# A message-passing kernel on one core: third parts of messages on another engine, an earlier x load, and normalisation in single steps

## The chip, the cores and the metric

The kernel runs on one core of a Trainium2 chip. The metric is the device time of one execution in microseconds. A core has TensorE (PE, matmuls; PEld is its weight load), VectorE (DVE), ScalarE (ACT), GpSimd (POOL) and SyncE (SP). The first four compute, each through its own queue in program order. SyncE, ScalarE and GpSimd issue the DMAs here.

## The reference

There are 6250 nodes with 128 features and 100000 edges, sorted by destination. Each edge has one of two types, and its message is the source row times one of two weight matrices plus a bias. Messages are summed at the destination, the node's own product is added, and ReLU, residual and a layer norm follow:

```
Xs = X[src]
m_data = Xs @ W_data.T + b_data
m_ctrl = Xs @ W_control.T + b_control
msg = jnp.where((edge_types == 0)[:, None], m_data, m_ctrl)
agg = jax.ops.segment_sum(msg, dst, num_segments=X.shape[0])
out = agg + (X @ W_self.T + b_self)
x = layernorm(x + relu(out))          # eps 1e-5, over 128 features
```

## The kernel before

**Table of messages.** Since a message depends only on source and type, the kernel computes all of them once. Nodes stand in 49 blocks of 128. For each block `multiply` (lines 457 to 466) makes y = x w + bias in fp32 in PSUM, 256 columns for the two types. Two blocks share a PSUM bank (a "pair", 25 in all), and four banks rotate. The f32 value is then split into three bf16 parts that add up to it: `take` (lines 471 to 474) copies the sum to bf16 on ScalarE, and `leave` (476 to 482) subtracts the copy from the PSUM sum on TensorE, with a matmul by minus the identity. So each pair goes y, yh (high copy), y1 (subtract), ym (middle copy), y2 (subtract), yl (low copy). Three copies of a pair on ScalarE and two subtractions for each block on TensorE are needed. The parts stay in SBUF as m3 and are stored to DRAM as table.

**Edges.** SyncE loads a sample of edges (r), from which VectorE, TensorE and a gather (er) find the first edge of each block. Then SyncE loads a window of edges for each block (line 372), after it has read the start from the tile first. Blocks are taken in two ways. The first 35, in seven groups of five, use selection by matmuls: `edge_fields` computes fields on VectorE, `bucket_hots` makes one-hot tiles hot_st (line 548), and in `ranks` TensorE and VectorE take turns for 18 steps: a matmul with tri, a max reduction into slot (line 565), a matmul with rest. `fill_a` and `fill_b` turn slots into lists (hr, two, then small at line 602). The lists go through DRAM (packed) and come back to all partitions as rows; VectorE compares them (line 727). From there TensorE gathers messages by matmuls with m3 (g_ps, line 756), ScalarE evicts them (gs, line 771) and TensorE adds them into agg by a one-hot matmul with hot_d. The other 14 blocks take their messages from the table by GpSimd's gathers (msg, line 857), which need all stores of the table; they are added into agg_g.

**Order.** `Order.run` is a planner that works while the program is built. Each stream yields steps with a price for each engine that may take it, and with needs. The planner puts the step that can start first, by due time, into the program. When a step has two engines, the one that would start first takes it. The prices and due times thus decide the order in which instructions stand in each engine's queue. On the chip the queues run by themselves.

**End of a block.** `finish_blocks` sums the three parts, adds x and takes statistics. `normalise` (from line 812) does this for a group of up to five blocks: square root on ScalarE, reciprocals on VectorE, then `apply` (lines 188 to 191), one ScalarE activation per block, all five as one step priced at 0.28 us each, and a store. `sums_over_all` is a fallback that runs only when the counts don't match all edges.

The loads at the start are bias and then w on ScalarE's queue (lines 241 and 243). x comes in seven parts (4, 8, 8, 8, 8, 8 and 5 blocks), through `load_x` on ScalarE's queue (line 452).

Of the kernel before, what the change touches and what calls it, by code (L numbers as in the profile page):

```python
# [9 lines left out]
F32 = mybir.dt.float32  # L10
# [9 lines left out]
P = 128  # L20
D = 128
# [79 lines left out]
def step(name, costs, *needs, lag=0.0):  # L101
    return as_tuple(name), costs, [as_tuple(n) for n in needs], lag
# [7 lines left out]
def kernel(  # L110
# [74 lines left out]
                                       op0=ALU.mult, op1=ALU.mult)  # L185
        return rstd, shift

    def apply(h, rstd, shift, n):
        for j in range(n):
            nc.scalar.activation(h[:, j, :], h[:, j, :], AF.Identity,  # L190
                                 bias=shift[:, j : j + 1], scale=rstd[:, j : j + 1])

    def store_out(h, b0, n, by=nc.sync):
        n0 = b0 * P
# [20 lines left out]
def sums_over_windows(ctx, tc, x, xt, edges, w, bias, table, packed, total,  # L215
# [21 lines left out]
    early = ctx.enter_context(ExitStack())  # L237
    build = early.enter_context(tc.tile_pool(name="build", bufs=2))
    ps_y = early.enter_context(tc.tile_pool(name="ps_y", bufs=YB, space=PSUM))
    b1 = build.tile([1, D3], F32, name="b1", bufs=1)  # L240
    A.dma_start(b1, bias)
    w_sb = const.tile([D, D3], F32, name="w_sb")
    A.dma_start(w_sb, w)


    iota_f = const.tile([P, 640], F32, name="iota_f")
# [46 lines left out]
        in_offset=bass.IndirectOffsetOnAxis(ap=row_i[:, 0:1], axis=0),  # L293
    )

    order.free.update(V=7.0, T=6.5, G=8.0)


    pid1 = const.tile([P, 1], F32, name="pid1")
# [74 lines left out]
            )  # L374


    xts, ys = {}, {}
    at_part = [sum(PARTS[:g]) for g in range(len(PARTS))]
    two_blocks = [(g, b, min(2, at_part[g] + n - b))
                  for g, n in enumerate(PARTS) for b in range(at_part[g], at_part[g] + n, 2)]  # L380


    LEAD, BUILT = 8.0, 76
    BLOCK = 13.1
    PACE = 1.68
    AHEAD, FIRST = 26.0, 20
# [60 lines left out]
    def load_x():  # L447
        for g, n in enumerate(PARTS):
            free = [("y", at_part[g - 1] - 1)] if g > 1 else []
            yield step(("xt", g), {"A": 0.45}, *free, lag=3.5)  # L450
            xts[g] = build.tile([D, max(PARTS), P], F32, name="xt")[:, :n]
            A.dma_start(xts[g].rearrange("p b c -> p (b c)"),
                        xt[:, at_part[g] * P : (at_part[g] + n) * P])

    def multiply():
        for i, (g, b, n) in enumerate(two_blocks):
            for j in range(n):
                free = [("yl", two_blocks[i - YB][1])] if i >= YB and j == 0 else []
                yield step(("y", b + j), {"T": 0.97}, ("xt", g), *free)
                if j == 0:  # L460
                    y = ys[b] = ps_y.tile([P, 2, 2 * D], F32, name="y")
                T.matmul(y[:, j, :], xts[g][:, b + j - at_part[g], :], w_sb[:, : 2 * D],  # L462
                         start=j == 0, stop=False, skip_group_check=True)
                T.matmul(y[:, j, :], ones_b, bias3[:, : 2 * D], start=False, stop=True, skip_group_check=True)  # L464
# [10 lines left out]
    def leave(i, kind, after):  # L475

        for g, b, n in two_blocks:
            yield step((kind, b), {"T": 0.11 * n}, (after, b))
            for j in range(n):
                T.matmul(ys[b][:, j, :].rearrange("p (t c) -> p t c", t=2), minus,  # L480
                         m3v[:, :, b + j, i * D : (i + 1) * D], start=False, stop=True,
                         skip_group_check=True)

    def store():
        for g, n in enumerate(PARTS):
# [305 lines left out]
    def own_of(blocks, begun):  # L791

        for i, b in enumerate(blocks):
            yield step(("agg", b), {"S": 0.0}, *([("whole", blocks[i - 1])] if i else []))
            yield step(("o", b), {"T": 0.5}, ("xs", b), begun(b))
            by_columns(aggs[b][:, :D], x_ts.pop(b), w_sb[:, 2 * D :], start=False, stop=False,
                       skip_group_check=True)
            by_columns(aggs[b][:, :D], ones_b, bias3[:, 2 * D :], start=False, stop=False,
                       skip_group_check=True)
# [16 lines left out]
    def normalise(pieces, last):  # L816

        for grp, (get, b0, q0, n) in enumerate(pieces):
            yield step((last, "root", grp), {"V": 0.2}, ("sum", b0 + n - 1))
            h, mv = get()  # L820
            h, mv = h[:, q0 : q0 + n, :], mv[:, q0 : q0 + n, :]
            v, s0 = root(mv, n, work)
            yield step((last, "rooted", grp), {"A": 0.3}, (last, "root", grp))
            yield step((last, "scale", grp), {"V": 1.0}, (last, "rooted", grp))
            scales = scale(mv, v, s0, n, work)
            yield step((last, "apply", grp), {"A": 0.28 * n}, (last, "scale", grp))
            apply(h, *scales, n)
            at_end = last == "p" and grp == len(pieces) - 1
            yield step((last, "out", grp), {"A": 0.4} if at_end else {"S": 0.3}, (last, "apply", grp))
            store_out(h, b0, n, nc.scalar if at_end else nc.sync)  # L830


# [75 lines left out]
    def close_build():  # L908
# [8 lines left out]
        spread(), select(), finish_blocks(),  # L917
        normalise([(lambda g=g: (hs_[g], mvs[g]), STARTS[g] + q0, q0, n) for g, q0, n in PIECES], "p"), add_up(), gather(), evict(), to_hots(), bucket_hots(),
        multiply(), take(0, "yh", "y"), leave(0, "y1", "yh"),
        take(1, "ym", "y1"), leave(1, "y2", "ym"), take(2, "yl", "y2"), constants(), store(), close_build(), add_counts(),  # L920
        finish_gathered(), gathered_sums(), gathered_hots(), gather_rows(), gathered_fields(),
        normalise([(lambda i=i: kept[i], NPB + i * GQ, 0, min(GQ, NG - i * GQ))
                   for i in range(-(-NG // GQ))], "g"),
# [8 lines left out]
def sums_over_all(ctx, tc, xt, edges, w, bias, table, dram, finish, load_rows, norm):  # L932
# [69 lines left out]
    for b0 in range(0, NB, Q):  # L1002
# [12 lines left out]
            finish(h[:, j, :], s_in, load_rows(b0 + j, work))  # L1015
            stats(mv[:, j, :], h[:, j, :], work)
        v, s0 = root(mv, n, work)
        apply(h, *scale(mv, v, s0, n, work), n)
        store_out(h, b0, n)


# [29 lines left out]
```

## Time and profile before

| | us |
|---|---|
| median of three runs | 545.55 |
| lowest, highest | 544.28, 546.7 |
| profiled execution | 628.27 |
| its span | 626.6 |
| TensorE busy in it | 550.4 |
| VectorE busy | 429.4 |
| ScalarE busy | 424.7 |
| GpSimd busy | 292.8 |

The profiled execution is longer than the runs by 82.7 us. Times inside the profile are from the start of the span. The start-up, in which the message parts and the first group's lists are made, ends when the first gather matmul starts, at 79.98 us. The main stage lasts from there to about 612 us, and the rest is the last group. In a line of a timeline the columns are start, duration, engine, line of the kernel, operation, output and inputs, shape and count; in brackets stands how long the engine was idle before it, and what released it.

### The profile page before, as it was taken

To read this page: it belongs to the slowest core of one execution; us is meant where nothing else is said; L and a number is where in the kernel's file an instruction comes from. 1 tells how busy PE (TensorE), PEld (TensorE's weight loads), DVE (VectorE), ACT (ScalarE), POOL (GpSimd) and SP (SyncE) were. 2 spreads that over 40 slices of the span, in tenths; PEclk is the share of its full clock that TensorE was granted. 3 is DMA by queue.
4 is the path that set the end of the run, shared out by engine and by line. 5 is a ranking of instruction groups with operands and counts; after the bars stand their busy time and mean duration, and the time that the engine had idled before them with its cause. 6 is when DMAs were issued, how large, how long until landed. Compare 5 with 4: busy or idle time off the path is not lost.

```text
span 626.6 us, 26397 instructions
## 1 busy us (share of the span) xinstructions
PE 550.4 (88%) x11222; PEld 441.2 (70%) x11222; DVE 429.4 (69%) x962; ACT 424.7 (68%) x1008; POOL 292.8 (47%) x267
## 2 busy tenths in 40 slices
PE   5899888896989898897988989999999998888994
PEld 3555466675768686786877877788777787666783
DVE  4767677567667777776787766877686667446784
ACT  6755555565587666777767676786767876676684
POOL 1000026654465556655556464665646554554400
PEclk9999988999899999999999999999999999999998
DMA  3567754324243433435333433443344542534300
GB/s 108 168 196 221 249 188 128 117 66 158 58 127 123 127 111 117 136 109 152 93 128 114 142 122 106 127 144 106 122 133 119 157 152 68 161 103 146 106 18 27
DMA packets 60932, 79.19 MB, mean 126 GB/s; under 512 B 15760, under 2 KB 51371, under 8 KB 60807
## 3 DMA queue, kind: packets, MB, share of 16 engines
q1 hardware_dynamic: 47109, 48.88, 24.3%
q0 software_dynamic: 12400, 25.08, 14.3%
q10 hardware_dynamic: 1298, 3.48, 1.6%
q8 instruction: 89, 1.46, 0.9%
q14 instruction: 36, 0.29, 0.1%
HBM read 64.35 MB, written 13.05 MB: 124 GB/s over the span
## 4 chain that ended last, share of the span: by engine, by line
PE 80%; ACT 7%; issue 5%; DVE 4%; DMA 2%; SPq 1%; another core or an unknown queue 0%; POOL 0%; ACTq 0%; DVEq 0%; POOLq 0%
PE agg L232 27%; PE g_ps L756 26%; PE acc L232 8%; PE agg_g L232 8%; PE small L602 7%; ACT gs L771 5%; PE y L462 2%; ACT h_p L190 1%; DMA rows<-packed 1%; DVE slot L565 1%; PE y L480 1%; DVE hot_st L548 1%; ACT h_g L190 1%; PE y L464 0%; DMA xt<-in_xt 0%
## 5 line engine op out<-in xcount | busy, mean ns | idle before, releaser
L771 ACT CAST gs<-g_ps 128x384 bf16<-128x384 f32 x804 | 337.2, 494 | 151.3 <-PE g_ps L756 97.4
L857 POOL DMA_INDIRECT msg<-table,idx x252 | 283.1, 1124 | 208.0 <-PE g_ps L756 90.5
L756 PE MATMUL g_ps<-m,rows 128*32 128x384 bf16 x3430 | 330.8, 334 | 19.2 <-ACT gs L771 11.6
L232 PE MATMUL agg<-gs,hot_d 128*32 128x384 bf16 x3360 | 304.4, 338 | 27.8 <-ACT gs L771 12.9
L232 PEld LDWEIGHTS <-hot_d 128*32 128x32 bf16 x3500 | 198.9, 137 | 66.7 <-issue 56.4
L756 PEld LDWEIGHTS <-rows 128*32 128x32 bf16 x3430 | 185.5, 138 | 46.4 <-issue 40.6
L565 DVE TENSOR_REDUCE slot<-acc 128x5 bf16<-128x490 f32 x126 | 83.8, 665 | 75.5 <-PE acc L232 39.7
L232 PE MATMUL agg_g<-msg,hot_g 128*32 128x384 bf16 x1008 | 107.2, 330 | 1.2 <-issue 1.1
L741 DVE TENSOR_TENSOR hot_d<-count,to 128x1664 bf16<-128x1664 bf16 x70 | 74.7, 1068 | 21.7 <-PE agg L232 12.8
L602 PE MATMUL small<-hot_st,two 128*32 128x98 bf16 x1260 | 70.9, 290 | 1.4 <-issue 1.3
L602 PEld LDWEIGHTS <-two 128*32 128x32 bf16 x1260 | 56.8, 118 | 6.7 <-issue 4.6
L232 PE MATMUL acc<-hot_st,rest 128*32 128x490 bf16 x476 | 55.1, 380 | 6.1 <-DVE slot L565 5.0
L232 PE MATMUL acc<-hot_st,tri 128*32 128x490 bf16 x504 | 58.8, 376 | 1.0 <-DVE hot_st L548 0.9
L473 ACT CAST m<-y 128x512 bf16<-128x512 f32 (+1 forms) x75 | 40.6, 580 | 25.7 <-PE y L480 18.0
L232 PEld LDWEIGHTS <-hot_g 128*32 128x32 bf16 x1008 | 51.4, 125 | 4.9 <-issue 3.0
L548 DVE TENSOR_TENSOR hot_st<-count,st_b 128x2940 bf16<-128x2940 bf16 x21 | 41.9, 1997 | 13.7 <-PE small L602 5.4
L696 POOL DMA_INDIRECT mixed<-table,row_i x7 | 7.4, 1055 | 87.3 <-PE g_ps L756 81.2
L727 DVE TENSOR_SCALAR rows<-rows,pid 128x3136 bf16<-128x3136 bf16 x35 | 36.3, 1038 | 3.3 <-DMA rows<-packed 3.3
L153 DVE TENSOR_REDUCE whole<-agg 128x128 f32<-128x384 f32 x35 | 19.4, 553 | 27.5 <-PE g_ps L756 23.4
L462 PE MATMUL y<-w_sb,xt 128*128 128x256 f32 x98 | 31.6, 409 | 1.7 <-DMA xt<-in_xt 1.7
L232 PEld LDWEIGHTS <-rest 128*32 128x32 bf16 x476 | 20.9, 99 | 16.0 <-issue 15.3
L771 DVE CAST gs<-g_ps 128x384 bf16<-128x384 f32 x36 | 19.3, 554 | 13.7 <-PE g_ps L756 12.2
(140 smaller groups left out, 423.6 us busy)
## 6 DMA issues: line engine op xcount, KB each, us to landing
rows<-packed SPq DMA_DIRECT2D x35, 784.0 KB
table<-m SPq DMA_DIRECT2D x10, 768.0 KB
msg<-table,idx POOLq DMA_INDIRECT x252
xt<-in_xt ACTq DMA_DIRECT2D x5, 512.0 KB
xt_p<-in_xt SPq DMA_DIRECT2D x35, 64.0 KB
xs_p<-in_x SPq DMA_DIRECT2D x35, 64.0 KB
out<-h_p SPq DMA_DIRECT2D x6, 320.0 KB
table<-m SPq DMA_DIRECT2D x2, 480.0 KB
```

Source lines behind the costliest of these rows:

```text
L153: nc.vector.tensor_reduce(whole, agg.rearrange("p (i c) -> p c i", i=3), axis=AX.X, op=ALU.add)
L232: T.matmul(out[c : c + 32], lhsT[:, c : c + 32], rhs, **flags)
L462: T.matmul(y[:, j, :], xts[g][:, b + j - at_part[g], :], w_sb[:, : 2 * D], start=j == 0, stop=False, skip_group_check=True)
L473: A.copy(part_of(b, n, i), ys[b][:, :n, :].rearrange("p b (t c) -> p t b c", t=2))
L548: V.tensor_tensor(hot, counted[n][:, None, 1 : NT + 1, :].to_broadcast([P, KC, NT, n]), fields[grp][2][:, c * KC : c * KC + KC, None, :].t ...
L565: V.tensor_reduce(slots[grp][:, k, :], by_q, axis=AX.X, op=ALU.max)
L602: T.matmul(vt[c0 : c0 + R, q // 2, :], two[:, k % KC, i, :, q], hot[:, k % KC, :, q], start=k == 0 and q < 2, stop=k == KT - 1, skip_group ...
L727: V.tensor_scalar(rows[b], rows[b], pid1, None, op0=ALU.is_equal)
L741: V.tensor_tensor(hot, counted[DC][:, :, :n], places[grp][:, q, None, c * DC : c * DC + n].to_broadcast([P, P, n]), op=ALU.is_equal)
L756: T.matmul(g_ps[t * R : (t + 1) * R, :D3], rows[b][:, :, s], m3[:, s, :], start=True, stop=True)
L771: (A.copy if e == "A" else V.tensor_copy)(gs[at], g_tiles.pop((b, g))[at, :D3])
L857: G.indirect_dma_start(out=msgs[j, k], out_offset=None, in_=table[:, :], in_offset=bass.IndirectOffsetOnAxis(ap=idx[:, j, k : k + 1], axis=0),
```

## The change

Four things are changed.

1. `leave` and `take` for the third part become `last_part`. For each pair the planner chooses. Either one VectorE tensor_sub reads the PSUM sum and the middle part and writes the third part, or, as before, TensorE subtracts and ScalarE copies. In the built program 9 of the 25 pairs go to VectorE.
2. The first part of x is loaded on SyncE's queue, second after r. w is loaded ahead of the bias on ScalarE's queue.
3. `apply` takes one block, and each one is a step of its own, priced at 0.39 us.
4. Prices and times of the planner: TensorE is free from 5.0 instead of 6.5, LEAD is 6.0 instead of 8.0, a y block costs 1.0 instead of 0.97, and a block's own product 0.25 instead of 0.5.

```
-    def apply(h, rstd, shift, n):
-        for j in range(n):
-            nc.scalar.activation(h[:, j, :], h[:, j, :], AF.Identity,
-                                 bias=shift[:, j : j + 1], scale=rstd[:, j : j + 1])
+    def apply(h, rstd, shift, j):
+        nc.scalar.activation(h[:, j, :], h[:, j, :], AF.Identity,
+                             bias=shift[:, j : j + 1], scale=rstd[:, j : j + 1])
...
+    w_sb = const.tile([D, D3], F32, name="w_sb")
+    A.dma_start(w_sb, w)
+    xts = {0: build.tile([D, max(PARTS), P], F32, name="xt")[:, : PARTS[0]]}
+    nc.sync.dma_start(xts[0].rearrange("p b c -> p (b c)"), xt[:, : PARTS[0] * P])
     b1 = build.tile([1, D3], F32, name="b1", bufs=1)
     A.dma_start(b1, bias)
-    w_sb = const.tile([D, D3], F32, name="w_sb")
-    A.dma_start(w_sb, w)
...
-    order.free.update(V=7.0, T=6.5, G=8.0)
+    order.free.update(V=7.0, T=5.0, G=8.0)
...
-    LEAD, BUILT = 8.0, 76
+    LEAD, BUILT = 6.0, 76
...
-            yield step(("xt", g), {"A": 0.45}, *free, lag=3.5)
+            yield step(("xt", g), {"A": 0.45} if g else {"S": 0.0}, *free, lag=3.5 if g else 0.0)
+            if not g:
+                continue
...
-                yield step(("y", b + j), {"T": 0.97}, ("xt", g), *free)
+                yield step(("y", b + j), {"T": 1.0}, ("xt", g), *free)
...
+    def last_part():
+
+        for g, b, n in two_blocks:
+            by = yield step(("y2", b), {"T": 0.11 * n, "V": 0.13 + 0.275 * n}, ("ym", b))
+            sums = ys[b][:, :n, :].rearrange("p b (t c) -> p t b c", t=2)
+            if by == "V":
+                V.tensor_sub(part_of(b, n, 2), sums, part_of(b, n, 1))
+            else:
+                for j in range(n):
+                    T.matmul(ys[b][:, j, :].rearrange("p (t c) -> p t c", t=2), minus,
+                             m3v[:, :, b + j, D : 2 * D], start=False, stop=True,
+                             skip_group_check=True)
+            yield step(("yl", b), {"A": 0.16 + 0.21 * n} if by == "T" else {"S": 0.0}, ("y2", b))
+            if by == "T":
+                A.copy(part_of(b, n, 2), sums)
...
-            yield step(("o", b), {"T": 0.5}, ("xs", b), begun(b))
+            yield step(("o", b), {"T": 0.25}, ("xs", b), begun(b))
...
-            yield step((last, "apply", grp), {"A": 0.28 * n}, (last, "scale", grp))
-            apply(h, *scales, n)
+            for j in range(n):
+                yield step((last, "apply", grp, j), {"A": 0.39}, (last, "scale", grp))
+                apply(h, *scales, j)
...
-        take(1, "ym", "y1"), leave(1, "y2", "ym"), take(2, "yl", "y2"), constants(), store(), close_build(), add_counts(),
+        take(1, "ym", "y1"), last_part(), constants(), store(), close_build(), add_counts(),
```

More of the change, by code (lines that the diff above doesn't have):

```diff
@@ L374, in starts @@
             )
-    xts, ys = {}, {}
+    ys = {}
     at_part = [sum(PARTS[:g]) for g in range(len(PARTS))]
@@ L825, in normalise @@
             scales = scale(mv, v, s0, n, work)
-            yield step((last, "apply", grp), {"A": 0.28 * n}, (last, "scale", grp))
-            apply(h, *scales, n)
+            for j in range(n):
+                yield step((last, "apply", grp, j), {"A": 0.39}, (last, "scale", grp))
+                apply(h, *scales, j)
             at_end = last == "p" and grp == len(pieces) - 1
-            yield step((last, "out", grp), {"A": 0.4} if at_end else {"S": 0.3}, (last, "apply", grp))
+            yield step((last, "out", grp), {"A": 0.4} if at_end else {"S": 0.3}, (last, "apply", grp, n - 1))
             store_out(h, b0, n, nc.scalar if at_end else nc.sync)
@@ L1017, in sums_over_all @@
         v, s0 = root(mv, n, work)
-        apply(h, *scale(mv, v, s0, n, work), n)
+        scales = scale(mv, v, s0, n, work)
+        for j in range(n):
+            apply(h, *scales, j)
         store_out(h, b0, n)
```

## The prediction

> **What bounds the kernel now.** I read the page first, then the chain of waits, then the start-up (the first 80 us) by timeline, because nearly all of the edit lies there.
>
> ```profile
> span 626.6 us, 26397 instructions
> PE 550.4 (88%) x11222; PEld 441.2 (70%) x11222; DVE 429.4 (69%) x962; ACT 424.7 (68%) x1008; POOL 292.8 (47%) x267
> PE 80%; ACT 7%; issue 5%; DVE 4%; DMA 2%; SPq 1%; another core or an unknown queue 0%; POOL 0%; ACTq 0%; DVEq 0%; POOLq 0%
> ```
>
> TensorE carries 80% of the chain that ended last, so work taken off another engine is worth only what TensorE waits for it. TensorE's own work that the edit removes is in the start-up. This is that stage in stretches of 10 us (columns: length, busy PE, PEld, DVE, ACT, POOL, granted clock, DMA share, GB/s):
>
> ```profile
> 10.00:20.00 10.00, 9.61 (x59) 6.86 (x58) 1.72 (x11) 8.00 (x17) 0.00 (x0) 1.00 0.48 133
> 20.00:30.00 10.00, 8.43 (x62) 5.19 (x60) 9.79 (x22) 6.88 (x14) 0.00 (x0) 1.00 0.55 154
> 40.00:50.00 10.00, 9.93 (x115) 5.62 (x113) 7.55 (x10) 6.71 (x12) 0.00 (x0) 1.00 0.75 229
> 70.00:80.00 10.00, 7.00 (x62) 3.45 (x64) 7.14 (x24) 4.88 (x10) 0.00 (x0) 0.95 0.87 290
> ```
>
> So three limits follow each other: from 18.4 to 30.7 us VectorE (9.79 of 10), then TensorE until 68, then, in 70 to 80, the DMA engines and VectorE, with TensorE idle 3 of 10. The timelines show both hand-overs. VectorE at the first and the last one, and TensorE's wait between:
>
> ```profile
> 18.41 0.32 DVE L515 TENSOR_TENSOR rel_b<-win,base 128x90 bf16<-128x90 int32 x1 [6.03 <-DMA win<-in_edges]
> 20.84 3.90 DVE L548 TENSOR_TENSOR hot_st<-count,st_b 128x2940 bf16<-128x2940 bf16 x2
> 32.78 0.67 DVE L565 TENSOR_REDUCE slot<-acc 128x5 bf16<-128x490 f32 x1 [0.73 <-PE acc L232]
> 75.18 1.04 DVE L727 TENSOR_SCALAR rows<-rows,pid 128x3136 bf16<-128x3136 bf16 x1 [1.58 <-DMA rows<-packed]
> 77.54 1.04 DVE L727 TENSOR_SCALAR rows<-rows,pid 128x3136 bf16<-128x3136 bf16 x1 [0.75 <-DMA rows<-packed]
> 78.50 0.66 DVE L565 TENSOR_REDUCE slot<-acc 128x5 bf16<-128x490 f32 x1
> ```
> ```profile
> 22.89 0.39 PE L232 MATMUL acc<-hot_st,tri 128*32 128x490 bf16 x4 [0.89 <-DVE hot_st L548]
> 79.21 0.60 PE L232 MATMUL acc<-hot_st,rest 128*32 128x490 bf16 x4 [1.44 <-DVE slot L565]
> ```
>
> The second fence says that the first rank matmul waits for VectorE, and that the last one before the gathers begin (first g_ps at 79.98) waits for a slot reduction which stands in VectorE's queue behind the selection of the second block's rows, and so behind a DMA.
>
> **What the Trainium skill says.** "VectorE: DVE Perf Modes", the TRN2 errata section and the perf-mode tier table: an operation from PSUM costs about 120 cycles plus its elements at 0.96 GHz, and tensor_tensor with a PSUM operand runs at one element a cycle. For 512 elements that is an estimate of 0.66 us. The trace is slightly above the formula: 490 elements from PSUM took 0.667 (formula 0.635), so I take 0.69, of which 0.62 shows as spacing. "DMA: Bandwidth & Descriptors", "Issuing engines are not separate DMA queues": moving a load to another issuing engine saves issue time only. The trace of before has no such pair to compare. [...] Here DMA traffic ends at about 86 us and the first table gather is issued at 88.32, 2.3 us later. "TensorE: Matmul & The Clock Gate", Part 1: the first 3.4 us or so of activity run at half clock. Here a y matmul pair goes from 0.85 us at 9.47 to 0.43 at 11.43, with the step near 10.5, 3.5 us after the start; an earlier start brings the same cold stretch with it.
>
> **The change part by part.** Sums are on the profiled execution, 628.27 us (span 626.6). The median of the runs shown is 545.55, 82.7 less, so profiling stretches the kernel; I carry absolute differences over, and scaled by 545.55/628.27 = 0.87 they would be a little smaller.
>
> x and w. The first x load leaves ScalarE's queue (issued at 4.16 behind the bias copies, landed 6.87) for SyncE's, behind the r load that takes 1.0 us to issue. With the 2.7 us that it took, it lands near 4.5 to 5.3; TensorE is held by begun until 4.92 + 0.3, so y starts at about 5.4 instead of 7.00. It is one DMA, and SyncE's next instruction is only at 12.4 (it waited 10.6 us for first), so nothing behind it is late. b now follows w in ScalarE's queue: about 0.4 us later, hence the parts on VectorE, begun, er. That is hidden: first_f was ready at 10.03 and first waited 2.15 us for TensorE's queue; without this cover +0.4. The 1.5 us head start goes into a wait: the first rank matmul already waits 0.89 us for hot_st. Worth 0; bounds -1.5 and +0.4.
>
> Two early subtractions. In the built program one stands on VectorE ahead of first, one between the fields and the first hot_st. The first needs the second pair's middle part; I place ScalarE's copy at 11.2 to 11.8, so first ends about 0.2 later. Behind it are SyncE's window loads and all of group 0. The second delays hot_st, on the chain, by 0.62. Together +0.8 (bounds 0 and +1.6).
>
> Fewer subtractions on TensorE. 9 of 25 pairs go to VectorE: 98 to 80 minus matmuls, 18 less. Between the rank step at 30.7 and the last L602 of group 0 there are 44 of them before and 32 after, with 21 y blocks in both. In the chain a pair is 0.22 alone and 0.32 next to acc, so 0.13 each: 12 x 0.13 = -1.6 (bounds -1.3, -1.9). The nine ScalarE casts that go (0.58 each) are hidden: ScalarE idles 25.7 us before its L473 casts.
>
> Five subtractions among the rank steps. Each takes 0.62 of VectorE; a step leaves VectorE idle 0.70 to 0.89 (0.73 above). They fit when their copy is there; one stands directly before hr and two (2.2 us), where nothing is idle. +0.4 (bounds 0 and +3). Slots ready, packed and the rows loads therefore: 0.8 - 1.6 + 0.4 = -0.4.
>
> The start of the gathers. In the new order the slot that the last rest needs, and also hr, two and the first hot_d, stand behind the first block's rows only; the second rows selection comes after two hot_d. Before: 77.54 + 1.04, slot 0.66, acc at 79.21. After: 75.18 + 0.95, slot, about 76.8. That is -2.4 for g_ps, and -2.3 for the first agg (hot_d ends at 80.0 instead of 82.3). What is late next: the gathered messages. POOL's table gathers begin at 88.32, when the stores have landed, msg 0 at 89.50; TensorE takes it at 92.72 and would now be there at 90.3. The DMA share is 0.9 to 1.1 from 72 to 86, so the stores don't land sooner. I credit -1.6 (bounds -2.4 and 0).
>
> Single normalisation steps. Five applies run together 2.04 us on ScalarE, ahead of evictions, and TensorE then waits 1.1 to 1.24 us (186.36, 264.13, 574.22). The planner's price goes from 0.28 to 0.39, the spacing that they have. In the built program evictions come between applies in four of the ten runs of five or four (1+4, 1+4, 1+1+2, 1+3); six runs of five stay whole, though planned. Three or four applies still stand together, so I take 0.3 for each of the four: -1.2 (bounds -3 and 0). The new prices of y and o and the earlier start add no instruction; they reorder TensorE by a few tiles: 0, bounds -2 and +2. The fallback's apply isn't executed.
>
> Sum: -0.4 - 1.6 - 1.2 = -3.2, so 628.3 becomes 625.1 profiled, and 545.55 becomes 542.3.
>
> **The rivals.** First: the message gathers take the place of the wait removed (the -1.6 becomes 0) and half the normalisation gain is lost: -0.4 - 0.6 = -1.0, about 544.6. For it: the 2.4 us between where TensorE would be and where it was. Against: TensorE in 90 to 98 is idle 3.4 of 8 us by "issue", which no gather explains. Second, on the other side: VectorE becomes the bound of the start-up. A subtraction waits for ScalarE's copy at the head of VectorE's queue, the slot behind it is late, then TensorE's rest and tri. Price: 9 x 0.62 = 5.6, less 1.6, so +4: 549.5. It decides once the copy is more than 0.1 us later than the slot before it, since 0.73 of idle less 0.62 is all there is. For it: DVE 9.79 of 10 in 20 to 30. Against: 7.55 in 40 to 50 leaves 2.5 us for about two subtractions. Third: the head start is kept, because y is further on at each rank step, and the gate and the applies give all that they have: -1.5, -0.8 and -1.8 more than the sum, about 538. The edit can't fail to do what it says: the built program shows nine subtractions and the moved load.
>
> **How the numbers follow.** Main case 45%, 542.3 (own range 539.5 to 544.5); gathers 20%, 544.6; VectorE bound 15%, 549.5; more gain 20%, 538. About 0.5%, 2.7 us, is what a measurement of this kernel can tell, so faster means under 542.8: somewhat over half of the main case and all of the last, 0.26 + 0.20 = 0.46. Same: the rest of the main case and nearly all of the gathers, 0.19 + 0.18 = 0.37. Slower: 0.15 + 0.02 = 0.17. The range leaves out part of both outer cases: 536.0 to 548.5.
>
> **What would show it.** First y matmul near 5.4; first rank matmul near 23.5 with a longer wait for hot_st; packed within 1 us of 68.8; first g_ps near 77 to 78; nine subtractions of 0.69. Wrong: slot reductions with waits for ScalarE casts ahead of them, TensorE under 9 of 10 between 30 and 68, a wait of 2 us at the first agg_g, or a main stage (80 to 612) that changes by more than 2 us either way.

## The result and the profile after

| | before | after |
|---|---|---|
| median of five runs, us | 546.52 | 542.67 |
| lowest, highest | 544.28, 546.7 | 542.34, 543.6 |
| ratio, 95% interval | | 0.9939 [0.9911, 0.9966] |

The medians are 3.85 us apart; the ratio of 0.9939 is 3.3 us (1.9 to 4.9). The forecast was 542.3. The total came out nearly as worked out, but most of its parts did not.

First a mistake about the profile of before. I had said that profiling stretches the kernel by 82.7 us. The changed kernel's profiled execution took 542.67 us, exactly its median:

```profile
span 540.9 us, 26355 instructions
PE 507.3 (94%) x11204; PEld 442.9 (82%) x11204; DVE 432.4 (80%) x967; ACT 415.9 (77%) x1003; POOL 297.4 (55%) x267
PE 73%; DMA 9%; ACT 5%; DVE 5%; issue 3%; SPq 3%; POOL 1%; ACTq 0%; DVEq 0%; POOLq 0%
```

So the profile doesn't stretch anything. In the experiments the kernel before, unprofiled, took 636.5 to 637.2 us on two chips, 630.4 on a third and 548.0 on a fourth. The first profile of before (628.27) is of the longer kind, the times shown beside it are of the shorter. Below, ratios are therefore always made on one chip, and the main stage is compared between profiles of one kind only. The start-up of one kernel takes the same time on all of them within 2 us (table below).

The start-up in the changed kernel's timeline (start, duration, engine, line, operation, tiles, shape, count, and in brackets the idle time before and what ended it), VectorE first, then TensorE:

```profile
3.36 0.35 DVE L272 CAST parts<-b 1x384 bf16<-1x384 f32 x1 [1.05 <-DMA b<-in_bias]
13.14 0.69 DVE L493 TENSOR_TENSOR m<-y,m 128x512 bf16<-128x512 f32 x1 [2.14 <-ACT m L476]
13.75 0.19 DVE L358 TENSOR_SCALAR first<-small 1x49 int32<-1x49 f32 x1
22.30 0.69 DVE L493 TENSOR_TENSOR m<-y,m 128x512 bf16<-128x512 f32 x1
22.90 3.90 DVE L567 TENSOR_TENSOR hot_st<-count,st_b 128x2940 bf16<-128x2940 bf16 x2
77.84 1.04 DVE L746 TENSOR_SCALAR rows<-rows,pid 128x3136 bf16<-128x3136 bf16 x1 [1.01 <-DMA rows<-packed]
78.79 0.67 DVE L584 TENSOR_REDUCE slot<-acc 128x5 bf16<-128x490 f32 x1
...
24.94 0.39 PE L231 MATMUL acc<-hot_st,tri 128*32 128x490 bf16 x4 [2.15 <-DVE hot_st L567]
79.51 0.39 PE L231 MATMUL acc<-hot_st,rest 128*32 128x490 bf16 x4 [1.94 <-DVE slot L584]
94.91 0.53 PE L231 MATMUL agg_g<-msg,hot_g 128*32 128x384 bf16 x4 [3.50 <-DMA msg<-table,idx]
```

The two early subtractions stand directly ahead of first (13.75) and of hot_st (22.90). The slot now waits for one selection of rows instead of two, as expected, but that selection comes at 77.84 and not at 75.18. The last line is the wait of the first rival: TensorE stands still for 3.50 us until the first gathered message has landed. Two of the stretches shown for before, in the changed kernel (length, busy PE, PEld, DVE, ACT, POOL, clock, DMA share, GB/s):

```profile
20.00:30.00 10.00, 7.58 (x42) 4.15 (x41) 9.86 (x19) 4.59 (x9) 0.00 (x0) 0.83 0.57 156
70.00:80.00 10.00, 7.02 (x69) 3.61 (x71) 8.45 (x28) 5.15 (x12) 0.00 (x0) 1.00 0.65 218
```

VectorE still sets the pace in 20 to 30 (9.86 of 10), and TensorE has lost 0.85 us there and some of its clock (0.83 granted). In 70 to 80 the DMA engines were busy 0.87 before and are now busy 0.65: something comes late to them.

One profile each would mislead here, because two executions of one kernel differ by up to 2.0 us within the start-up. This table has three of each, from several chips. The right-hand ones are two of the changed kernel and one of a version with the same start-up (applies joined, below).

| start, us | before | mean | changed start-up | mean | moved |
|---|---|---|---|---|---|
| parts | 2.24, 2.23, 2.24 | 2.24 | 3.36, 3.12, 3.10 | 3.19 | +0.96 |
| first y matmul | 7.00, 6.89, 6.96 | 6.95 | 6.05, 5.81, 5.79 | 5.88 | -1.07 |
| first | 12.18, 11.94, 12.81 | 12.31 | 13.75, 12.88, 13.04 | 13.22 | +0.91 |
| first rank matmul | 22.89, 22.68, 23.74 | 23.10 | 24.94, 24.13, 24.17 | 24.41 | +1.31 |
| lists ready (vs) | 66.71, 66.46, 67.59 | 66.92 | 68.72, 67.27, 67.94 | 67.98 | +1.06 |
| packed issued | 68.80, 68.98, 69.86 | 69.21 | 69.27, 67.98, 68.69 | 68.65 | -0.57 |
| rows issued | 70.36, 70.56, 71.43 | 70.78 | 72.54, 71.81, 72.34 | 72.23 | +1.45 |
| first g_ps | 79.98, 80.00, 81.29 | 80.42 | 79.92, 78.40, 78.90 | 79.07 | -1.35 |
| first msg gather | 89.50, 89.76, 90.61 | 89.96 | 91.54, 90.88, 91.41 | 91.28 | +1.32 |
| first agg_g | 92.72, 92.88, 94.70 | 93.43 | 94.91, 93.55, 94.22 | 94.23 | +0.79 |

The lists of the first group are ready when ScalarE copies them to vs, and packed is their store. Around these two the order of time is, in the kernel before and in the changed one:

```profile
66.71 0.32 ACT L615 CAST vs<-small 128x196 bf16<-128x196 f32 x1 [2.74 <-PE small L602]
68.27 0.44 SPq L158 DMA_DIRECT2D xs_p<-in_x  x1
68.80 0.85 SPq L620 DMA_DIRECT2D packed<-vs  x2
```
```profile
68.72 0.32 ACT L634 CAST vs<-small 128x196 bf16<-128x196 f32 x1
69.27 1.47 SPq L639 DMA_DIRECT2D packed<-vs  x2
```

Read downwards the table tells the story. 1.1 us are won at y, 2.0 lost from there to first, and 0.4 more by the first rank matmul. From there to the lists only 0.25 us are won. The 1.6 that packed then seems to win are SyncE's: in the kernel before its queue was still busy with loads of x, and packed was issued 1.6 to 2.1 us after the copies to vs had ended, now 0.1 to 0.3. These 1.6, and 0.4 more, are lost between packed and rows. 2.8 are won from there to g_ps, and 2.1 lost again by the first agg_g. So the lead of 1.35 us at g_ps is spent: as far as three profiles each can tell, whose first agg_g differ by up to 2.0 us, the first agg_g comes no earlier than before. By this the 3.3 us must come from behind it.

### The profile page after: what moved, and what is told of

Same layout as the page of the kernel before. It is cut to its first block, busy times and chain, and to the rows that moved or that the text cites. A ratio compares the mean times of both kernels' runs of the same rounds, so it can differ in the third digit from the quotient of the medians.

```text
span 540.9 us, 26355 instructions
## 1 busy us (share of the span) xinstructions
PE 507.3 (94%) x11204; PEld 442.9 (82%) x11204; DVE 432.4 (80%) x967; ACT 415.9 (77%) x1003; POOL 297.4 (55%) x267
## 4 chain that ended last, share of the span: by engine, by line
PE 73%; DMA 9%; ACT 5%; DVE 5%; issue 3%; SPq 3%; POOL 1%; ACTq 0%; DVEq 0%; POOLq 0%
PE agg L231 25%; PE g_ps L775 23%; PE acc L231 8%; PE agg_g L231 7%; PE small L621 6%; DMA msg<-table,idx 5%; ACT gs L790 2%; DMA rows<-packed 2%; PE y L465 2%; SPq L807 1%; POOL msg L877 1%; ACT h_p L189 1%; SPq L158 1%; DVE slot L584 1%; DVE hot_st L567 1%
## 5 line engine op out<-in xcount | busy, mean ns | idle before, releaser
L790 ACT CAST gs<-g_ps 128x384 bf16<-128x384 f32 x807 | 333.7, 498 | 72.4 <-PE g_ps L775 53.5
L877 POOL DMA_INDIRECT msg<-table,idx x252 | 288.5, 1145 | 115.4 <-PE g_ps L775 46.4
L775 PE MATMUL g_ps<-m,rows 128*32 128x384 bf16 x3430 | 322.4, 332 | 0.9 <-ACT gs L790 0.7
L231 PEld LDWEIGHTS <-hot_d 128*32 128x32 bf16 x3500 | 195.8, 137 | 13.1 <-issue 7.1
L775 PEld LDWEIGHTS <-rows 128*32 128x32 bf16 x3430 | 189.8, 137 | 18.5 <-issue 12.7
L231 PE MATMUL acc<-hot_st,tri 128*32 128x490 bf16 x504 | 61.8, 376 | 2.1 <-DVE hot_st L567 2.1
L231 PEld LDWEIGHTS <-hot_g 128*32 128x32 bf16 x1008 | 53.5, 123 | 10.6 <-issue 7.8
L476 ACT CAST m<-y 128x512 bf16<-128x512 f32 (+1 forms) x50 | 28.1, 577 | 30.9 <-PE y L483 23.1
L231 PEld LDWEIGHTS <-rest 128*32 128x32 bf16 x476 | 22.1, 98 | 12.8 <-issue 11.8
L231 PEld LDWEIGHTS <-tri 128*32 128x32 bf16 x504 | 22.4, 99 | 3.3 <-issue 3.1
```

The lines of the kernel that those rows point to most:

```text
L231: T.matmul(out[c : c + 32], lhsT[:, c : c + 32], rhs, **flags)
L476: A.copy(part_of(b, n, i), ys[b][:, :n, :].rearrange("p b (t c) -> p t b c", t=2))
L775: T.matmul(g_ps[t * R : (t + 1) * R, :D3], rows[b][:, :, s], m3[:, s, :], start=True, stop=True)
L790: (A.copy if e == "A" else V.tensor_copy)(gs[at], g_tiles.pop((b, g))[at, :D3])
L877: G.indirect_dma_start(out=msgs[j, k], out_offset=None, in_=table[:, :], in_offset=bass.IndirectOffsetOnAxis(ap=idx[:, j, k : k + 1], axis=0),
```

## The experiments

The theories named in the expectations are M (the gain is in the main stage, by the single normalisation steps), S (in the start-up), P (in the order that the planner makes, since any new price or step plans everything after it anew) and C (only where the kernel before takes 546 us).

### One part alone, added to the kernel before

First the kernel before itself once more, as the measure of what a ratio near 1 means.

> The kernel before, unchanged, for a second profile. The profiled execution of before took 628.3 us and its runs 546; that of after took 542.7, as its runs. If the first profile was an outlier, this one is near 547 with a main stage of about 13 us a block, and its start-up (to the first g_ps at 79.98 us) is within 1 us of the first profile's. Ratio 1.000 within 0.003 by every theory.

Measured: 1.0003 [0.9979, 1.0028], 636.9 us.

Single applies alone:

```
-            yield step((last, "apply", grp), {"A": 0.28 * n}, (last, "scale", grp))
-            apply(h, *scales, n)
+            for j in range(n):
+                yield step((last, "apply", grp, j), {"A": 0.39}, (last, "scale", grp))
+                apply(h, *scales, j)
```

> Before, with single normalisation steps alone. Theory M (the gain lies in the main stage and comes from the applies being priced at 0.39 and let apart): 543 to 544, the whole gain. Theory S (the gain comes from the start-up, as predicted in part): 545.3, the 1.2 us of the forecast. Theory P (any new order of the plan moves the time by some us, and the gain belongs to no one edit): anything from 541 to 548.

Measured: 1.0034 [1.0017, 1.0052], slower by 2.2 us. In its profile the first g_ps starts at 82.67 and the first agg_g at 97.42, 4.5 us later than in the kernel before on the same chip (92.88): the new prices moved work of the start-up, although no apply is in it.

The third parts alone:

```
-        take(1, "ym", "y1"), leave(1, "y2", "ym"), take(2, "yl", "y2"), constants(), ...
+        take(1, "ym", "y1"), last_part(), constants(), ...
```

> Before, with the third part by VectorE or in two steps alone. Theory S: 544 to 545, and the first g_ps earlier than 79.98 us. Theory M: 546 to 548, with first g_ps at 80 or later, since the subtractions ahead of first and hot_st delay the rank steps. Theory P: 541 to 548.

Measured: 0.9986 [0.9967, 1.0005]. Here the planner gave 14 pairs to VectorE, and the first g_ps came at 83.72. The reason is in SyncE's queue. This is what it issues there, first in the kernel before, then in the changed one, then with the third parts alone:

```profile
53.56 5.97 SPq L490 DMA_DIRECT2D table<-m  x4
68.98 0.85 SPq L620 DMA_DIRECT2D packed<-vs  x2
70.56 2.02 SPq L720 DMA_DIRECT2D rows<-packed  x3
```
```profile
62.48 1.00 SPq L509 DMA_DIRECT2D table<-m  x2
69.27 1.47 SPq L639 DMA_DIRECT2D packed<-vs  x2
72.54 1.29 SPq L739 DMA_DIRECT2D rows<-packed  x3
73.92 8.05 SPq L509 DMA_DIRECT2D table<-m  x3
```
```profile
70.09 1.01 SPq L506 DMA_DIRECT2D table<-m  x2
71.20 2.54 SPq L636 DMA_DIRECT2D packed<-vs  x2
78.42 1.29 SPq L736 DMA_DIRECT2D rows<-packed  x3
82.63 1.04 DVE L743 TENSOR_SCALAR rows<-rows,pid 128x3136 bf16<-128x3136 bf16 x1 [7.08 <-DMA rows<-packed]
```

The loads of rows wait until packed has landed. With the last two stores of table (768 KB each) 11 us ahead of packed, from packed to rows takes 1.6 us; with them 6.8 us ahead it takes 3.3; with them 1.1 us ahead it takes 7.2. Of the versions below, the one with the planner's old figures also has them 1.1 us ahead, and 7.0 us; the one with the early pairs left on TensorE has them 7.0 us ahead, and 2.0 us. The time rises as the stores come nearer. Other loads differ between these plans too, so this compares plans; no run moves the stores alone. The fourth line of the second fence says what is late next: the last stores of table stand behind the rows in SyncE's queue, and the message gathers need all stores.

The head alone (x on SyncE, w ahead of the bias, TensorE free from 5.0):

```
+    A.dma_start(w_sb, w)
+    xts = {0: build.tile([D, max(PARTS), P], F32, name="xt")[:, : PARTS[0]]}
+    nc.sync.dma_start(xts[0].rearrange("p b c -> p (b c)"), xt[:, : PARTS[0] * P])
     A.dma_start(b1, bias)
-    A.dma_start(w_sb, w)
```

> Before, with w ahead of the bias, the first x load on SyncE's queue and TensorE planned free from 5.0 alone. Forecast: 546.5, no change, because the earlier y only makes the first rank matmul wait longer. The trace of after says worse: parts on VectorE start at 3.36 instead of 2.24, and er is issued at 6.80 instead of 5.94; if that reaches first (12.2 before), the time is about 547.4. Theory P: 542 to 549.

Measured: 1.0000 [0.9974, 1.0026]. Behind the start-up TensorE's order is here that of the kernel before. y starts at 5.67, 1.3 us earlier than the mean of before, and first at 12.72, 0.4 us later. Worth nothing within 1.7 us either way, as forecast.

No part alone gives the gain. The sum of the three is +1.3 us by their ratios.

### The changed kernel again, and its parts taken away

> The changed kernel once more, beside the kernel before on the same chip. All numbers are ratios to that. If the gain belongs to the kernel (theories M: single normalisation steps in the main stage, S: start-up, P: the order that the planner chooses): 0.992 to 0.996, and on a chip where the kernel before takes about 637 us some 633 to 635. Since none of three parts alone moved the time by more than 0.34% there, a sum of the parts would be 1.0002 (+2.3 - 0.4 - 0.5 us). If the gain is one that exists only where the kernel before takes 546 us (theory C, the condition of the chip): 0.998 to 1.003 where it takes 637.

Measured: 0.9973 [0.9955, 0.999], 634.5 against 636.5 us. So there is a gain on this chip too, perhaps a smaller one: 1.7 us, and the interval just overlaps that of the first measurement. It leaves out 1, so a gain that exists only where the kernel before takes 546 us falls; but 0.9973 lies between the ranges named for C and for the others, and the interval reaches into both. A sum of the parts (1.0020) falls as well.

With the applies of a group as one step at the old price, all else as changed:

```
-            for j in range(n):
-                yield step((last, "apply", grp, j), {"A": 0.39}, (last, "scale", grp))
-                apply(h, *scales, j)
+            yield step((last, "apply", grp), {"A": 0.28 * n}, (last, "scale", grp))
+            apply(h, *scales, n)
```

> The changed kernel with the applies of a group in one step at the old price of 0.28 us each. Theory M: the gain goes, ratio to before 0.998 to 1.001, so some 3 us above the changed kernel on the same chip. Theory S: as the changed kernel, within 0.5 us. Theory P: anything within 3 us either side of the changed kernel, and then TensorE's order differs in the main stage. From the part alone, which cost 2.3 us on the chip with 637 us: 2 us below the changed kernel there.

Measured: 1.0187 [1.0161, 1.0213], 647.6 us, 13.1 above the changed kernel. None of the theories had named such a number; P had allowed 3. At the first agg_g it is 1.3 us behind (94.83 for 93.55), so most of the loss lies in the main stage. The granted clock in its runs is 0.971 in the median and 0.978 in those of the changed kernel. Among the changed kernel's own 22 runs 0.01 of clock goes with some 3 us, so by this estimate the clock accounts for 2 of the 13 us.

With the planner's old figures (TensorE stays planned free from 5.0):

```
-    LEAD, BUILT = 6.0, 76
+    LEAD, BUILT = 8.0, 76
-                yield step(("y", b + j), {"T": 1.0}, ("xt", g), *free)
+                yield step(("y", b + j), {"T": 0.97}, ("xt", g), *free)
-            yield step(("o", b), {"T": 0.25}, ("xs", b), begun(b))
+            yield step(("o", b), {"T": 0.5}, ("xs", b), begun(b))
```

> The changed kernel with the old figures of the planner (LEAD 8.0, y 0.97, o 0.5). Theory P with these prices as its cause: the gain goes, ratio to before about 1.000 (the sum of the three parts alone). Theories M and S: as the changed kernel, within 0.7 us.

Measured: 1.0042 [1.0015, 1.0068]. The gain goes, as P says, by 4.7 us against the changed kernel, which is more than P's 1.000. Its profile shows one place that is large enough. With the old figures the planner gives 16 pairs to VectorE instead of 9 and puts two stores of table 1.1 us ahead of packed; rows follow packed after 7.0 us, the first g_ps comes at 87.47, and the first agg_g at 98.76, 5.2 us after the changed kernel's on the same chip (93.55). So this loss can be one of the start-up, by the stores, and doesn't tell of the main stage's order.

And those figures alone, as new ones, in the kernel before (the same three lines the other way round):

> The kernel before with only the new figures of the planner (LEAD 6.0, y 1.0, o 0.25). Theory P with these prices as its cause: 0.993 to 0.996. Theories M and S: 0.999 to 1.001, since no instruction is added or removed.

Measured: 1.0172 [1.0151, 1.0192], 646.5 us. No work is added or removed; the order changes, and a few evictions go from VectorE to ScalarE (VectorE has 959 instructions instead of 962). It costs 10 us, of which 2.3 are there at the first agg_g (95.17 for 92.88). The direction is the opposite of what P expected.

Put into the kernel before, the new figures cost 10 us and single applies 2.2. Everything but the single applies is 11 to 12 us slower than the kernel before, and with everything there is a gain. What the edit brings is not a sum over its parts. A stretch that stands out, in the kernel before and then with the new figures alone (the same columns as above, then the longest of TensorE's waits in that stretch):

```profile
320.00:330.00 10.00, 9.54 (x218) 8.21 (x216) 8.79 (x17) 6.99 (x17) 6.41 (x6) 1.00 0.35 96
```
```profile
320.00:330.00 10.00, 6.84 (x92) 4.55 (x88) 4.43 (x15) 3.92 (x9) 5.03 (x5) 0.70 0.45 144
...
PEld L756 <- issue: 4.2, 4, 2.2
```

92 matmuls instead of 218, with waits for nothing that the profile shows ("issue", 4.2 us at the weight load) and with a clock of 0.70. Over the whole program the second of these profiles is 13.9 us longer: TensorE is busy 8.3 us longer (562.6 for 554.3) with the same 11222 matmuls, and idle 5.6 us longer. The granted clock of the runs is 0.980 in the median, and 0.982 in the kernel before, so the clock as a whole doesn't account for it. What in the order does was not found.

### Start-up alone, at a fixed order

Now versions that leave the main stage's order untouched. In the first, TensorE's instructions are those of the changed kernel from about the 190th on; the early pairs keep their matmuls, and the bias goes ahead of w again:

```
-            by = yield step(("y2", b), {"T": 0.11 * n, "V": 0.13 + 0.275 * n}, ("ym", b))
+            by = yield step(("y2", b), {"T": 0.11 * n} if b < 16 else {"T": 0.11 * n, "V": 0.13 + 0.275 * n}, ("ym", b))
...
+    A.dma_start(b1, bias)
     A.dma_start(w_sb, w)
-    A.dma_start(b1, bias)
```

> The changed kernel without the two early VectorE subtractions (the pairs below block 16 keep their matmuls) and with the bias load ahead of w again, x still on SyncE. Theory S (the start-up sets the gain): the first rank matmul comes back from 24.9 us to 22.0 to 23.0, packed from 69.3 to 67 to 68.5, first g_ps to 77.5 to 79, and the time falls 1 to 2.5 us below the changed kernel on the same chip. Theory P (the order of the main stage sets it): the start-up comes forward as said, but the end doesn't follow it; anything within 4 us either side of the changed kernel, since every later step is planned anew. Rival that TensorE's work until 68 us is the bound whatever the start: first rank matmul earlier, packed within 0.5 us of 69.3, time within 0.7 us of the changed kernel.

Measured: 0.991 [0.9882, 0.9938], 625.0 against 630.4 us. Its timeline:

```profile
2.23 0.34 DVE L272 CAST parts<-b 1x384 bf16<-1x384 f32 x1
11.54 0.20 DVE L358 TENSOR_SCALAR first<-small 1x49 int32<-1x49 f32 x1 [1.45 <-PE small L356]
20.27 3.90 DVE L567 TENSOR_TENSOR hot_st<-count,st_b 128x2940 bf16<-128x2940 bf16 x2
...
22.32 0.39 PE L231 MATMUL acc<-hot_st,tri 128*32 128x490 bf16 x4 [1.60 <-DVE hot_st L567]
91.50 0.54 PE L231 MATMUL agg_g<-msg,hot_g 128*32 128x384 bf16 x4 [3.45 <-DMA msg<-table,idx]
```

The first rank matmul is 1.81 us earlier than in the changed kernel's own profile of this kind (24.13), the lists 1.81 (65.46 for 67.27), the first g_ps 1.87 (76.53 for 78.40), the first agg_g 2.05 (93.55). A head start at first passes through the whole start-up, even through the wait for the messages, because the stores and the gathers move with it. Against the changed kernel's 0.9973 the ratio is 0.9937, with the two intervals combined 0.990 to 0.997, or 4.0 us (1.9 to 6.1). The 2 us seen in the start-up are within that. The two ratios are from two chips of the longer kind, since the versions were not run side by side; against the 0.9939 of the shorter kind it would be 1.6 us and not certain. This version beats the kernel before, and by the first comparison the changed kernel too.

Only the bias ahead of w, TensorE's order the same throughout:

```
+    A.dma_start(b1, bias)
     A.dma_start(w_sb, w)
-    A.dma_start(b1, bias)
```

> The changed kernel with only the bias load put ahead of w again on ScalarE's queue; x stays on SyncE's, and TensorE's order is the same instruction for instruction. Theory S: parts on VectorE at 2.2 in place of 3.4 us, first at 12.6 to 12.9 in place of 13.4 to 13.8, first rank matmul 1.0 us earlier than in the changed kernel, and all of it kept until the gathers: the time 0.8 to 1.2 us below the changed kernel, the other 0.7 to 1.0 us of the version without the two early subtractions being theirs. The prediction's step (0.4 us later, hidden by a wait of 2.15 us for TensorE's queue): as the changed kernel, within 0.4 us.

Measured: 0.9895 [0.9852, 0.9938], 542.2 us where before takes 548.0. Against 0.9939 that is 0.9956, 0.990 to 1.001: 2.4 us, not certain (two chips of the shorter kind). The timeline:

```profile
2.23 0.34 DVE L272 CAST parts<-b 1x384 bf16<-1x384 f32 x1
12.46 0.19 DVE L358 TENSOR_SCALAR first<-small 1x49 int32<-1x49 f32 x1
23.78 0.53 PE L231 MATMUL acc<-hot_st,tri 128*32 128x490 bf16 x4 [2.28 <-DVE hot_st L567]
93.67 0.38 PE L231 MATMUL agg_g<-msg,hot_g 128*32 128x384 bf16 x4 [3.46 <-DMA msg<-table,idx]
```

parts is back at 2.23; first comes 0.76, the first rank matmul 0.63 and the first agg_g 0.56 us before the means of the table. The first two lie outside the three values of the changed start-up, the last one within them. So the bias behind w costs about 0.6 us by the first rank matmul. In this execution another gather was then waited for 2.74 us at 102.5, so the profile can't say that these 0.6 us reach the end.

### Single steps alone, at a fixed order

TensorE's order is again the same instruction for instruction. ScalarE only emits the applies of a group together, where the first one stands:

```
             for j in range(n):
                 yield step((last, "apply", grp, j), {"A": 0.39}, (last, "scale", grp))
-                apply(h, *scales, j)
+                for k in range(n) if not j else ():
+                    apply(h, *scales, k)
```

> The changed kernel with the order of every other engine as it is (TensorE's is the same instruction for instruction), but ScalarE emits the applies of a group together where the first of them stands: runs of 5, 5, 4 and 4 in place of 1+4, 1+4, 1+1+2 and 1+3. It parts what the single steps do themselves from what their new prices do to the order. The prediction's step (single steps themselves are worth 1.2 us, bounds 0 and 3): 0.9 to 1.6 us above the changed kernel on the same chip. Theory P (it is the planned order): as the changed kernel, within 0.5 us, and the kernel with grouped steps and its own order, 13 us slower than the changed one there, lost nearly all of it by its order.

Measured: 0.9976 [0.9954, 0.9998]. Against 0.9939 that is 1.0037 (1.000 to 1.007), 2.0 us slower than the changed kernel (0.1 to 3.9, again by two chips of the shorter kind). The time alone doesn't exclude P's 0.5 us; the profiles help. TensorE's waits (in total, times, longest) in the changed kernel, then with the applies joined, with three places of the latter's timeline at which an apply run is no longer broken up and the wait is about 1 us:

```profile
PE agg L231 <- ACT gs L790: 3.3, 6, 1.0
```
```profile
PE agg L231 <- ACT gs L790: 5.4, 7, 1.0
PE agg L231 <- ACT mixed L790: 1.1, 1, 1.1
...
365.06 0.39 PE L231 MATMUL agg<-gs,hot_d 128*32 128x384 bf16 x4 [1.04 <-ACT gs L790]
524.96 0.39 PE L231 MATMUL agg<-mixed,hot_d 128*32 128x384 bf16 x4 [1.15 <-ACT mixed L790]
532.75 0.39 PE L231 MATMUL agg<-gs,hot_d 128*32 128x384 bf16 x4 [1.01 <-ACT gs L790]
```

At the four places where a run is broken up, the waits in the changed kernel and here are 0.77 and 1.04, 0.21 and 1.04, none shown and 1.15, none shown and 1.01. The differences add up to 0.27 + 0.83 + 1.15 + 1.01 = 3.26 us, which is what separates the lines shown (6.5 and 3.3). From the first agg_g to the end the two profiles take 446.0 and 449.4 us. So the single steps themselves are worth 2 to 3 us. Against the kernel before, 1.3 us (0.1 to 2.5) are left for all the rest.

### The kernel before, once more

A profile of it from where it takes 546 us was wanted, to compare the main stages.

> The kernel before once more, for a profile of it from where it takes about 546 us, since its profile so far is from where it takes 628 to 637. Ratio 0.998 to 1.002. Theory S (the gain lies in the start-up): the main stage from the first message gather to the end is as long as in the changed kernel within 1 us, and the first agg_g of the changed kernel is earlier. Theory P or the single steps: the first g_ps and the first agg_g at the times of the changed kernel within 1 us, and the main stage 3 to 4 us longer than the changed kernel's, with TensorE's waits for ScalarE's casts longer by 2 us or more in all.

Measured: 0.9991 [0.9969, 1.0014], but at 637.4 us. Its profile is the third of the table above, and the main stage of before at 546 us has not been seen.

## Why the prediction was right, and where it was not

**The time.** 542.3 was forecast and 542.67 measured. That the total fits so closely is luck, because two errors cancelled: the start-up was to give 2.0 us and gave none (first agg_g at +0.8), and the single steps gave more than 1.2.

**x and w.** "Worth 0; bounds -1.5 and +0.4" was too kind. Two sizes failed. The bias was to be 0.4 us later, but parts moved by 0.96 in the mean: in the changed kernel the bias is issued at 1.23, behind w at 0.82, which is 0.41, and the rest is in the landing. And the cover, first waiting 2.15 us for TensorE's queue, moved too, because TensorE begins with begun, which stands behind the parts in VectorE's queue. So y started at 5.88 and not at 5.4. With the bias ahead, parts is at 2.23 and y at 5.00. The cost is about 0.6 us, beyond the bound. The rest of the head start went into TensorE's queue: ahead of the matmul for which first waits the plan now puts six blocks of y and six subtractions, and before it put five and two. So that matmul starts at 12.44 in the mean and not at 12.03, though y began 1.1 us earlier. (The two y pairs quoted for the clock start at 9.27 and 11.27, not at 9.47 and 11.43.)

**Two early subtractions.** The mechanism was right. hot_st starts 2.91 us after rel_b, and 2.43 in the kernel before: 0.48 for the second, where I had 0.62. first starts 0.79 us after its matmul instead of 0.28: 0.51 for the first, where I had 0.2, since it waits for ScalarE's copy. The sum is 1.0 against 0.8.

**Fewer subtractions on TensorE, five among the rank steps.** -1.6 and +0.4, together -1.2, was forecast by the time of packed. From the first rank matmul to packed the means shrink from 46.11 to 44.24, but 1.6 of that is SyncE's queue. To the lists it is 43.82 and 43.56 (43.78, 43.14, 43.77), so this term gave 0.25. The twelve subtractions are gone (44 for 56 in that stretch), and TensorE is busy for less time there: 41.72, 40.41 and 41.72 us, and 42.42 before. But its idle time rose from 1.4 to between 2.1 and 2.7, and in the two profiles with 43.8 the granted clock was 0.96 in the stretch (1.00 in the other). I had taken the removed work as time won, with no price for new waits. The fitting of VectorE's subtractions into its idle time holds. Nine run, of 681 ns in the mean (0.69 was taken, and 0.66 was the estimate from "VectorE: DVE Perf Modes" of the Trainium skill, its TRN2 errata), and only two wait for a copy (2.14 and 0.26 us). The second rival, VectorE as the bound, did not come about. "packed within 1 us of 68.8" holds, but by SyncE's queue, which hid that the lists were later.

**The start of the gathers.** The new place of the second selection gave 2.8 us from rows to g_ps, where 2.4 was forecast. What stands ahead of it failed: rows were to be issued 0.4 us earlier and are 1.45 later. 1.06 of this is the later lists. The other 0.4 is a DMA that moves: from the copy to vs to rows takes 4.25 instead of 3.86, because the plan puts two stores of the table 4 us later, to 6.8 us before packed, and packed lands late behind them. I had left such stores out. So g_ps gained 1.35 by the means and not 2.8. Then the credit of 1.6 was to survive the messages, and it didn't. The first rival had the right place, the first agg_g, and the wait is 3.50 to 3.65 us in all three; 2 us there was named as a sign of being wrong. But the gathers didn't just stay where they were, they moved 1.3 us later, by the same late rows: SyncE issues the last table stores behind them. From the numbers of before I had argued that "the stores don't land sooner"; that they land later followed from the order in SyncE's queue, which I had not followed to its end.

**Single steps.** The four breaks are there and the wait was the right one. The size failed: 0.3 us for each, 1.2 together, when they are 0.27, 0.83, 1.15 and 1.01. I had scaled the gain by the one apply that moves, but the cast that TensorE waits for is the one let through, so nearly the whole wait can go.

**Planner's prices.** "0, bounds -2 and +2" was right for the whole only by the company it kept. On a chip where before takes 637 us the prices alone cost 10 us, while the changed kernel loses 4.7 us without them. A bound on a new order taken from "a few tiles" has no ground in the profile. What remains of the measured 3.3 us after +0.8 at the start-up's end and 2.0 to 3.3 for the single steps is 0.8 to 2.1 us, and only the new order is left to account for it. That is a remainder, not shown, and within the intervals it can be nothing: the main stage of before was never seen where it takes 546 us.

**The profile's length.** "Profiling stretches the kernel" was wrong, as said; it didn't hurt, since the sum was made in absolute differences.

## What to carry to other kernels

When a planner decides the order, a changed price is a change of every queue behind it: hold the order fixed and change the instructions alone, or the reverse, before crediting a part with anything. A store that moves counts like an instruction that moves: a small transfer on which the next stage waits took 1.6, 3.3 or 7.2 us to become usable, and the longer the nearer two large stores were issued ahead of it. Before crediting a stage with an earlier hand-over, look when its result was ready and when the queue that passes it on came to it: 1.6 us of the gain at packed was the queue's. And a gain ahead of a wait for gathered data counts only if it moves the last store that the gather needs.

## What the runs showed of the hardware

One program takes 546 to 548 us on some chips and 630 to 637 on others. The single instructions are as long (in 200 to 300 us, g_ps 330 and 333 ns, its cast 497 and 493), but TensorE is less busy: the changed kernel from 200 to 300 us, first where it takes 542.7, then where it takes 634.5 us:

```profile
200.00:300.00 100.00, 97.61 (x2370) 89.24 (x2365) 88.31 (x210) 83.89 (x212) 70.42 (x63) 1.00 0.48 149
```
```profile
200.00:300.00 100.00, 88.84 (x1902) 71.95 (x1900) 69.42 (x150) 68.84 (x171) 58.41 (x50) 1.00 0.40 120
```

2370 matmuls become 1902 at a full clock. The idle time of weight loads put down to "issue", in 120 to 610 us, is 25.6 us in the first and 104.9 in the second. What the chips differ in was not tried. It also means that the size of an effect of order, such as the 10 us of the prices, is shown for one kind of chip only.

The second thing is when TensorE's clock steps up. The kernel before, in two executions (a pair of y matmuls takes 1.06 us ahead of the step and 0.60 behind it):

```profile
10.23 0.63 PE L462 MATMUL y<-w_sb,xt 128*128 128x256 f32 x2
11.66 0.24 PE L355 MATMUL small<-ident,first_f 49*1 49x49 f32 x2
```
```profile
10.29 1.06 PE L463 MATMUL y<-w_sb,xt 128*128 128x256 f32 x2
11.79 0.70 PE L463 MATMUL y<-w_sb,xt 128*128 128x256 f32 x2
12.53 0.24 PE L356 MATMUL small<-ident,first_f 49*1 49x49 f32 x2
```

In the first the step is at 10.2, in the second at about 11.8, with y begun at 6.89 and 6.96. The matmul ahead of first is 0.87 us later in the second, and so is first (12.81 for 11.94), the first g_ps by 1.3 (81.29 for 80.00) and the first agg_g by 1.8. The Trainium skill ("TensorE: Matmul & The Clock Gate", Part 1), which the prediction used, has the step after some 3.4 us of activity and says that it varies by about half a microsecond from run to run. From the first y matmul on these runs have 3.3 and 4.8, a wider spread. In the three profiles of the changed start-up the first faster pair starts 3.8, 5.0 and 5.3 us after the first y matmul, so an earlier start didn't bring the step forward by as much, against what the prediction had said. Two single profiles of the start-up can differ by more than the edit in question.
